# Holding SyncE's transfers back by bytes underway in a four-layer graph kernel

## The chip, the cores and the metric

The kernel runs on one core of a Trainium2 chip. A core has five engines that run side by side and meet at semaphores: TensorE (PE in the profile; its weight loads are PEld), VectorE (DVE), ScalarE (ACT), GpSimd (POOL) and SyncE (SP). Here SyncE does nothing but issue DMA transfers. The metric is device time in microseconds (us); lower is better.

## The reference

There are 128 graphs of 64 nodes with 512 features, so x is 8,192 rows of 512 float32. Four layers follow each other, and each ends in `x = layernorm(x + layer(x, adj))`:

```python
# layer 0: attention over the adjacency, output A @ x @ w
s = (x @ w) @ a;  A = leaky(tanh((s_i + s_j) / 8) * 8);  A = exp(A) * adj, rows scaled
# layer 1: weight = adj * exp(q k^T), rows divided by their sum; output weight @ v
# layer 2: softmax over the nodes of sum(q * (adj @ k)), times v
# layer 3: two hypergraph convolutions with 512 -> 1024 -> 512 features,
#          relu and layernorm between them
```

The weights are the same for all graphs: 512 x 512 for layers 0 to 2 and 512 x 1024, 1024 x 512 for layer 3.

## The kernel before

**Tiles and groups.** Two graphs make a tile of 128 rows, two tiles (`GT`) a group; there are 32 groups (`NG`). `run(g)` adds all operations of group g, in steps 0 to 15: layer 0 in steps 0 to 2, layer 1 in 3 to 6, layer 2 in 7 to 11, layer 3 in 12 to 15. A product with a weight is made of seven block products in place of eight (`seven_products`, Strassen's scheme in Winograd's form). For this each weight is prepared once into seven quarter-size pieces, which are stored in DRAM (`in_dram`), and every group streams them back (`streamed`): w0 for layer 0, v1 and v2 (both "ring<-v" in the profile) for layers 1 and 2, 3a and 3b for layer 3. The pieces go through a ring of eight buffers of 512 KB (kind `ring`). With x, the adjacency and the output this makes some 14 MB a group.

**The planner.** No engine's order is written by hand. The operations are put into a planner (class `Order`), each with an engine, a cost, a key (when it is due) and the buffers that it reads and writes. `Order.run` then plays through the program with its own model of times: an engine that is free takes the ready operation with the smallest key that finds free buffers, and a buffer is taken when its operation starts and is given back when the last one that touches it ends. The order that comes out is what is emitted, engine by engine; on the chip only the semaphores of the data count, not the planner's times. Four groups are worked on at a time (`BASE`, 4 of 16 steps apart), so TensorE has other groups' matmuls to turn to.

TensorE's operations come in the modes "whole" (the array of 128 x 128), "quarters" and "columns" (64 x 64 blocks, divided array), and "any". `choose` prefers to stay in a mode, since a change costs time.

**SyncE in the planner.** A transfer costs SyncE 500 ns (`dma`). A common link moves 300 bytes in a ns, one transfer after another, and 2,200 ns after its end the data counts as landed. The list `landed` keeps these times. When eight transfers are underway (`UNDERWAY`), SyncE is free again only when the eighth from the newest has landed. An operation of SyncE whose key is more than `AHEAD` beyond the earliest unfinished step isn't taken yet.

The key of a ring load is the smallest step of its users less 1.5. x and the adjacency have keys 6 and 7 below their group's base (`load_x`, `load_adj`), so they go out as soon as a buffer of theirs is free. `load_adj` makes one transfer of the adjacency as it is and four small ones that turn it (32 KB each). `load` tells the planner a size of 2 * P * 1024, 256 KB, whatever it loads.

**Waits on the chip.** Each of SyncE's transfers adds to one of eight semaphores, in turn, and waits first for what used the same semaphore before; so on the chip too it can't have more than eight underway. Other waits of SyncE are for buffers: a ring load waits for the matmuls that read its buffer last.

There is one wait that the data doesn't ask for. [...] Where the planner starts a GpSimd operation, it notes in `o.behind` the VectorE operation that had the port before. When the order is emitted, `pinned` gives the next instruction a real wait (a manual dependency of the kind Sync) on the instruction named in the list `behind`, and a NoSync one that fixes its place behind the last of its own engine. `names` remembers the instruction of each operation that could be waited for.

Of the kernel before, what the change touches and what calls it, by code (L numbers as in the profile page):

```python
# [16 lines left out]
P = 128  # L17
B, N, D, DH = 128, 64, 512, 1024
T = B * N // P
GT = 2  # L20
NG = T // GT
CT = 4
# [36 lines left out]
class Order:  # L59
    LATENCY = {"PE": 220, "DVE": 70, "ACT": 60, "POOL": 60, "SP": 2200}  # L60
    BYTES_PER_NS = 300
    UNDERWAY = 8
    TURN, TURN_DIVIDED = 145, 60

    NEAR, FAR = 0.8, 4.0
# [72 lines left out]
    def run(self):  # L138

        ready = {e: [] for e in self.LATENCY}  # L140
        free_at = {e: 0 for e in self.LATENCY}
        number = {o: i for i, o in enumerate(self.ops)}
        events, n, link, mode, burst = [], 0, 0, None, 0
        port_free, port_user, landed = 0, None, []
        for o in self.ops:
            if not o.missing:
                heappush(ready[o.engine], (o.key, number[o], o))
        by_step, front = sorted((o for o in self.ops if o.engine != "SP"), key=lambda o: o.step), 0
        done, now = [], 0
        while len(done) < len(self.ops):  # L150
            moved = False
            while front < len(by_step) and by_step[front].start is not None:
                front += 1
            far = by_step[front].step + self.AHEAD if front < len(by_step) else float("inf")
            for e, heap in ready.items():
                while free_at[e] <= now:
                    skipped, held, found, found_pe = [], set(), None, {}
                    while heap:
                        if e == "SP" and heap[0][0] > far:
                            break  # L160
                        item = heappop(heap)
                        need = defaultdict(int)
                        wants = [b for b in item[2].touches if b.slot is None]
                        for b in wants:
                            need[b.kind] += 1
                        if item[2].port and port_free > now:
                            skipped.append(item)
                        elif all(k not in held and len(self.slots[k]) >= c for k, c in need.items()):
                            if e == "PE":
                                skipped.append(item)  # L170
                                found_pe.setdefault(item[2].mode, []).append((item, wants))
                                if item[0] < 0:
                                    break
                            else:
                                found, takes = item, wants
                                break
                        else:
                            held.update(k for k, c in need.items() if k in held or len(self.slots[k]) < c)
                            skipped.append(item)
                    if found_pe:  # L180
                        found, takes = self.choose(found_pe, mode, burst)
                        skipped.remove(found)
                    for item in skipped:
                        heappush(heap, item)
                    if found is None:
                        break
                    moved, found = True, found[2]
                    turn = 0
                    if e == "PE":
                        if found.mode == "any":  # L190
                            found.mode = "whole" if mode in ("whole", None) else "quarters"
                            found.args = (found.mode == "whole",)
                        if found.mode != mode:
                            turn = self.TURN if "whole" in (found.mode, mode) else self.TURN_DIVIDED
                        mode = found.mode
                        burst = 0 if mode == "whole" else burst + found.matmuls
                    found.start = now
                    done.append(found)
                    found.takes = takes
                    for b in takes:  # L200
                        b.slot = self.slots[b.kind].pop()
                    end = free_at[e] = now + found.cost + turn
                    if found.port:
                        port_free = end
                        if e == "POOL":
                            found.behind = port_user
                        else:
                            port_user = found
                    if e == "SP":
                        link = max(link, now) + found.bytes // self.BYTES_PER_NS  # L210
                        end = max(end, link)
                        landed.append(end + self.LATENCY[e])
                        if len(landed) >= self.UNDERWAY:
                            free_at[e] = max(free_at[e], landed[-self.UNDERWAY])
                    seen = end + self.LATENCY[e]
                    heappush(events, (free_at[e], n, None, None))
                    for u in found.users:
                        n += 1
                        heappush(events, (free_at[e] if u.engine == e and e != "SP" else seen, n, u, None))
                    for b in found.touches:  # L220
                        n += 1
                        heappush(events, (seen, n, None, b))
                    n += 1
            if not events:
                stuck = [(e, h[0][2].key, [b.kind for b in h[0][2].touches]) for e, h in ready.items() if h]
                raise RuntimeError(f"no operation can start: {len(done)} of {len(self.ops)}, {stuck}")
            now = max(now, events[0][0])
            while events and events[0][0] <= now:
                _, _, u, b = heappop(events)
                if u is not None:  # L230
                    u.missing -= 1
                    if not u.missing:
                        heappush(ready[u.engine], (u.key, number[u], u))
                if b is not None:
                    b.left -= 1
                    if not b.left:
                        self.slots[b.kind].append(b.slot)
        return done
# [19 lines left out]
def kernel(  # L258
# [74 lines left out]
    def dma(size, reads, writes, out, in_):  # L333
        order.add("SP", 500, reads, writes, lambda: nc.sync.dma_start(out=out(), in_=in_()), size=size)

    def load(b, src, view=None):
        dma(2 * P * 1024, [], [b], lambda: view(b.t) if view else b.t, lambda: src)

    NOW = 100.0

# [40 lines left out]
    def load_x(g):  # L381
        order.key = BASE[g] - 6.0 if g else -11.0
        xs[g] = Buf("x", 4)
        load(xs[g], x_g[g])

    def load_adj(c):
        order.key = BASE[GC * c] - 7.0 if c else -10.5
        adjs[c] = Buf("adj")
        load(adjs[c], adjT[:, ts(c, CT * N)], lambda t_: t_.rearrange("p t i -> p (t i)"))

        turned = turned_adjs[c] = Buf("adj", 2 * GT)
        for t in range(GT):
            for h in range(2):
                dma(P * 256, [], [turned[2 * t + h]],
                    lambda t=t, h=h: turned.t[ts(t, N)].rearrange("p (g h) i -> p g h i", h=2)[:, :, h],
                    lambda t=t, h=h: adjT_c[c, t][:, :, h])
# [753 lines left out]
    def pinned(engine):  # L1150
        class Pinned:
            def __getattr__(self, name):
                f = getattr(engine, name)

                def call(*args, **kwargs):
                    made = f(*args, **kwargs)  # L1156
                    ins = made.ins
                    key = str(ins.engine)
                    if behind:
                        tc.add_manual_dep(ins, behind.pop(), mybir.DependencyInfo(  # L1160
                            mybir.DependencyClass.Sync, mybir.DependencyReason.DATA), reason="port")
                    if key in last:
                        tc.add_manual_dep(ins, last[key], mybir.DependencyInfo(
                            mybir.DependencyClass.NoSync, mybir.DependencyReason.DATA), reason="order")
                    last[key] = ins.name
                    return made

                return call

        return Pinned()  # L1170
# [7 lines left out]
    for o in order.run():  # L1178
# [2 lines left out]
        if o.behind:  # L1181
            behind.append(names[o.behind])
        o.emit(*o.args)
        if o.port and o.engine == "DVE":
            names[o] = last[str(mybir.EngineType.DVE)]


# [39 lines left out]
```

## Time and profile before

| | |
|---|---|
| median of three runs | 2173.8 us (2173.52 to 2175.92) |
| the profiled execution | 2173.7 us |
| its span, first to last instruction | 2171.8 us |
| mean granted clock of TensorE | 0.997 |
| TensorE busy | 2141.3 us (99%) |
| VectorE, ScalarE, GpSimd busy | 70%, 39%, 18% |
| transfers issued by SyncE | 1,067 |
| moved by DMA | 476 MB, 219 GB/s in the mean |
| share of time that the DMA engines were busy with them | 65.4% |

The busy time of TensorE is made of matmuls whose ends are modelled, so a gap of some 0.1 us between two of them can hide in it. A group of rows names an instruction by what it writes and reads, "bank<-ring,k" being a matmul into a PSUM bank with a ring piece and a buffer of kind k. All instructions carry line 1156, since one helper (`pinned`) emits them. A wait is put down to the engine or transfer whose semaphore came last. "Issue" is time in which the engine waited for nothing that the profile shows.

### The profile page before, as it was taken

The numbers are of one execution on the slowest core, as the hardware profiler recorded it, in microseconds if no ns is written. First come the engines' busy times: TensorE is split into PE (matmuls) and PEld (weight loads), VectorE is DVE, ScalarE is ACT, GpSimd is POOL, SyncE is SP. The second block draws the span as 40 slices with busy tenths as digits, with TensorE's granted clock in tenths as the row PEclk, the third lists the DMA queues.
The fourth block names the chain that finished last, engine by engine and source line by source line (L and its number), as shares of the span: only waits on it lengthen the run. The fifth ranks groups of instructions, "written<-read, shape, count | busy, mean of one in ns | idle before, by whom it ended". The sixth has DMA issues, their size and how long they took to land.

```text
span 2171.8 us, 51970 instructions
## 1 busy us (share of the span) xinstructions
PE 2141.3 (99%) x21079; PEld 1727.3 (80%) x21079; DVE 1531.0 (70%) x3967; ACT 853.1 (39%) x1812; POOL 384.9 (18%) x399
## 2 busy tenths in 40 slices
PE   8999999999999999999999999999999999999998
PEld 4888787887888887877888788878877888888866
DVE  5777767677677777667676676777766767666775
ACT  2444344343343443433433334433434333343333
POOL 1113111021210222201121111212112221012120
PEclk9999999999999999999999999999999999999999
DMA  9776668666666667665666665676656676656475
GB/s 304 232 258 229 210 211 271 213 234 232 216 229 204 205 210 231 233 210 196 205 222 235 210 200 196 220 237 217 223 194 204 222 236 212 210 185 211 158 260 188
DMA packets 174303, 476.38 MB, mean 219 GB/s; under 512 B 35760, under 2 KB 45296, under 8 KB 174064
## 3 DMA queue, kind: packets, MB, share of 16 engines
q1 hardware_dynamic: 174064, 473.05, 65.4%
q8 instruction: 167, 2.74, 0.5%
q14 instruction: 72, 0.59, 0.1%
HBM read 443.33 MB, written 29.66 MB: 218 GB/s over the span
## 4 chain that ended last, share of the span: by engine, by line
PE 99%; issue 1%; DVE 0%; DMA 0%; ACT 0%; SPq 0%; DVEq 0%; ACTq 0%
PE bank L1156 99%; DMA k<-in_wk_dram 0%; DVE col L1156 0%; ACT x L1156 0%; DVE x L1156 0%; ACT k L1156 0%; ACT u_b L1156 0%; SPq L1156 0%; DVE e L1156 0%; DVEq L1156 0%; ACTq L1156 0%
## 5 line engine op out<-in xcount | busy, mean ns | idle before, releaser
L1156 PE MATMUL bank<-ring,k 128*128 128x256 f32 (+1 forms) x3968 | 1037.0, 410 | 5.2 <-issue 4.0
L1156 PEld LDWEIGHTS bank<-ring,k 128*128 128x128 f32 x3968 | 735.1, 191 | 194.9 <-issue 95.3
L1156 DVE SCALAR_TENSOR_TENSOR x<-bank,col,x 128x256 f32<-128x256 f32 (+1 forms) x832 | 399.8, 500 | 223.2 <-PE bank L1156 213.9
L1156 ACT COPY k<-bank 128x512 f32<-128x512 f32 (+1 forms) x640 | 301.6, 503 | 450.0 <-PE bank L1156 363.6
L1156 PEld LDWEIGHTS bank<-k,m 128*128 128x128 f32 x3584 | 429.9, 192 | 23.9 <-issue 10.5
L1156 PE MATMUL bank<-k,m 128*128 128x128 f32 x3584 | 437.1, 275 | 0.0
L1156 PE MATMUL bank<-ring,h 128*128 128x256 f32 (+1 forms) x1408 | 418.4, 439 | 0.0
L1156 POOL TENSOR_TENSOR col<-col,mhalf 128x2 f32<-128x2 f32 (+1 forms) x161 | 111.6, 694 | 1414.1 <-DVE col L1156 913.7
L1156 ACT ACTIVATE x<-x,col,col 128x512 f32<-128x512 f32 x256 | 196.0, 814 | 373.0 <-DVE col L1156 372.9
L1156 PEld LDWEIGHTS bank<-ring,h 128*128 128x128 f32 x1408 | 257.4, 190 | 85.7 <-issue 60.5
L1156 DVE TENSOR_TENSOR k<-bank,k 128x256 f32<-128x256 f32 x384 | 154.0, 421 | 149.4 <-PE bank L1156 147.5
L1156 DVE BATCH_NORM_STATS2 col<-x 128x6 f32<-128x512 f32 x256 | 175.5, 688 | 4.7 <-ACT k L1156 0.3
L1156 ACT ACTIVATE k<-bank,u_c 128x128 f32<-128x128 f32 x256 | 80.3, 366 | 151.0 <-PE bank L1156 140.8
L1156 DVE SCALAR_TENSOR_TENSOR h<-bank,col,b3a_b 128x512 f32<-128x512 f32 x128 | 95.8, 748 | 54.4 <-PE bank L1156 54.2
L1156 DVE TENSOR_TENSOR k<-k 128x256 f32<-128x256 f32 x226 | 103.6, 459 | 34.0 <-ACT k L1156 31.8
L1156 ACT ACTIVATE h<-h 128x512 f32<-128x512 f32 x128 | 80.4, 631 | 107.1 <-DVE h L1156 106.9
L1156 PEld LDWEIGHTS bank<-k,k 128*64 128x64 f32 (+1 forms) x2112 | 77.3, 140 | 51.5 <-DVE k L1156 25.2
L1156 DVE SCALAR_TENSOR_TENSOR h<-bank,col,h 128x512 f32<-128x512 f32 x128 | 93.3, 747 | 31.0 <-PE bank L1156 30.8
L1156 PE MATMUL bank<-k,k 128*64 128x64 f32 (+1 forms) x2112 | 105.5, 238 | 7.0 <-DMA k<-in_wk_dram 6.3
L1156 ACT ACTIVATE h<-h,col,col 128x512 f32<-128x512 f32 x128 | 94.8, 804 | 44.0 <-DVE col L1156 44.0
L1156 POOL TENSOR_TENSOR x<-x,bv_b 128x512 f32<-128x512 f32 x64 | 80.8, 1272 | 107.3 <-PE bank L1156 95.2
L1156 POOL TENSOR_TENSOR k<-k,b3b_b 128x512 f32<-128x512 f32 x64 | 81.4, 1271 | 87.8 <-DVE h L1156 31.1
(98 smaller groups left out, 1493.9 us busy)
## 6 DMA issues: line engine op xcount, KB each, us to landing
ring<-3a SPq DMA_DIRECT2D x224, 512.0 KB, 4.8
ring<-3b SPq DMA_DIRECT2D x224, 512.0 KB, 4.7
ring<-v SPq DMA_DIRECT2D x189, 512.0 KB, 4.2
ring<-w SPq DMA_DIRECT2D x93, 512.0 KB, 3.3
x<-in_x_dram SPq DMA_DIRECT2D x32, 512.0 KB, 4.0
ring<-v SPq DMA_DIRECT2D x63, 256.0 KB, 4.2
out_dram<-x SPq DMA_DIRECT2D x31, 512.0 KB, 5.0
ring<-w SPq DMA_DIRECT2D x31, 256.0 KB, 4.0
```

The costliest lines, as they stand in the source:

```text
L1156: made = f(*args, **kwargs)
```

## The change

Four things are altered.

1. In the planner a second limit stands beside the eight transfers: `BYTES`, 3 << 19, which is 1.5 MB. After each transfer the planner walks back from the newest, starting from 512 KB (1 << 19) for the transfer to come, and adds up sizes. At the first transfer that brings the sum over 1.5 MB, or at the eighth, it stops: SyncE is free again when that one has landed.
2. If it stopped for the bytes, the transfer found is kept in `behind`, and the next transfer of SyncE gets it as `found.behind`. When that one is emitted it has a real wait for the landing, by the way that GpSimd's wait already had. For this `names` keeps SyncE's instructions too.
3. `load` is given the true size: 512 KB for x (P * GT * D * 4), 128 KB for the adjacency (P * CT * N * 4), in place of 256 KB for both.
4. The text that tells the reason of a manual dependency reads "turn" in place of "port".

The planner runs anew with this, so the order of operations on all engines may come out differently.

```diff
-    UNDERWAY = 8
+    UNDERWAY, BYTES = 8, 3 << 19
...
-        port_free, port_user, landed = 0, None, []
+        port_free, port_user, landed, behind = 0, None, [], None
...
                     if e == "SP":
                         link = max(link, now) + found.bytes // self.BYTES_PER_NS
                         end = max(end, link)
-                        landed.append(end + self.LATENCY[e])
-                        if len(landed) >= self.UNDERWAY:
-                            free_at[e] = max(free_at[e], landed[-self.UNDERWAY])
+                        landed.append((end + self.LATENCY[e], found))
+                        found.behind, behind, size = behind, None, 1 << 19
+                        for i, (at, o) in enumerate(reversed(landed), 1):
+                            size += o.bytes
+                            if i == self.UNDERWAY or size > self.BYTES:
+                                free_at[e], behind = max(free_at[e], at), o if i < self.UNDERWAY else None
+                                break
...
-    def load(b, src, view=None):
-        dma(2 * P * 1024, [], [b], lambda: view(b.t) if view else b.t, lambda: src)
+    def load(b, src, size, view=None):
+        dma(size, [], [b], lambda: view(b.t) if view else b.t, lambda: src)
...
-        load(xs[g], x_g[g])
+        load(xs[g], x_g[g], P * GT * D * 4)
...
-        load(adjs[c], adjT[:, ts(c, CT * N)], lambda t_: t_.rearrange("p t i -> p (t i)"))
+        load(adjs[c], adjT[:, ts(c, CT * N)], P * CT * N * 4, lambda t_: t_.rearrange("p t i -> p (t i)"))
...
-                            mybir.DependencyClass.Sync, mybir.DependencyReason.DATA), reason="port")
+                            mybir.DependencyClass.Sync, mybir.DependencyReason.DATA), reason="turn")
...
-        if o.port and o.engine == "DVE":
-            names[o] = last[str(mybir.EngineType.DVE)]
+        if o.engine == "SP" or o.port and o.engine == "DVE":
+            names[o] = last[str(mybir.EngineType.SP if o.engine == "SP" else mybir.EngineType.DVE)]
```

## The prediction

> **What bounds the kernel now.** I read the busy times first, then who TensorE waited for, then SyncE's waits, then SyncE's order around the places where the hold would act.
>
> ```profile
> PE 2141.3 (99%) x21079; PEld 1727.3 (80%) x21079; DVE 1531.0 (70%) x3967; ACT 853.1 (39%) x1812; POOL 384.9 (18%) x399
> ```
>
> TensorE is busy for 99% of the span; 30.5 us are left. The waits of TensorE from 54 us to the end, after the start-up (waiting engine, releaser: us in total, times, longest):
>
> ```profile
> PE bank L1156 <- issue: 13.3, 10, 2.3
> PE bank L1156 <- ACT k L1156: 1.1, 1, 1.1
> PE bank L1156 <- ACT x L1156: 0.2, 1, 0.2
> ```
>
> No transfer is in it (the 1.1 us is one that spills over from 52.84 us). So after the start no matmul is late because of a DMA. The ten waits on "issue" come with the fetch of TensorE's own instructions: each begins between 0.1 us before and 1.6 us after the start of a 16 KB transfer of the instruction queue, and ends 2.2 to 3.0 us after that start. Who SyncE waited for:
>
> ```profile
> SPq L1156 <- PE bank L1156: 1514.0, 772, 11.7
> SPq L1156 <- DMA out_dram<-x: 86.8, 21, 5.7
> ```
>
> For 70% of the span SyncE stands ready and waits until TensorE gives back a ring buffer. Its transfers, KB each and median us to landing:
>
> ```profile
> ring<-3a SPq DMA_DIRECT2D x224, 512.0 KB, 4.8
> ring<-3b SPq DMA_DIRECT2D x224, 512.0 KB, 4.7
> ring<-v SPq DMA_DIRECT2D x189, 512.0 KB, 4.2
> ring<-w SPq DMA_DIRECT2D x93, 512.0 KB, 3.3
> ```
>
> And the one place where TensorE's idle time is in reach of an order of transfers, the end of the start-up:
>
> ```profile
> 51.43 1.41 PE L1156 MATMUL bank<-e,x 64*64 64x64 f32 x64 [1.92 <-DVE e L1156]
> 53.98 2.50 PE L1156 MATMUL bank<-ring,k 128*128 128x256 f32 x5 [1.15 <-ACT k L1156]
> ```
>
> These two waits, 3.1 us, are followed by a clock of one half from 52.2 to 59.0 us: eleven matmuls stand there 0.21 us further from the next than elsewhere, 2.3 us. VectorE and ScalarE end the waits.
>
> **What the Trainium skill says.** "DMA: Bandwidth & Descriptors", Queues, rings and completion order: each DMA engine takes one queue's descriptors in ring order. The trace agrees: the first six 512 KB loads were issued within 3.4 us and landed at 4.79, 6.13, 7.49, 8.84, 10.20 and 11.55 us, one every 1.35 us. The same page, Anatomy of one DMA: a fixed cost of about 2 us lies mostly after the last byte. Here 22 ring loads of 512 KB into an empty queue took 3.19 us (median), which leaves 1.8 us beside the 1.35 us. "Runtime: NRT & Kernel Launch", Instruction fetch mechanics: an engine fetches pages of 256 instructions while it runs the one before. The trace has 167 such transfers and 42,826 weight loads and matmuls, 256 to each.
>
> **The hold itself.** By the new rule SyncE counts 512 KB ahead, then adds transfers from the newest back. With 512 KB each that is 1.0, 1.5, 2.0 MB: the third from the newest must land before the next goes out, so three are underway. Three take 3 x 1.35 = 4.05 us of the queue, and one alone needs 3.19 us, so the queue should not run dry. I applied the rule to the 1,067 issue and landing records. At 308 issues the named transfer had not landed. Moving those issues, and what follows them on SyncE, holds 249 transfers for 237 us in all, but landings move by 0.04 us in the mean and 1.3 us at most, because a transfer that is held would only have stood in the queue. Behind the waiting instruction stand the next loads on SyncE, and TensorE waits for these.
>
> Does anything notice? I laid the kernel's program order of matmuls on the records (all 21,079 match), which gives for each load the time from landing to its first matmul. Of 804 ring loads after 108 us one has 1.1 us (a 3a piece of 177 us), then come 1.6 us and up; 7 more are under 2 us, and all those are first pieces of 3b in a group; ring<-v has a median of 14.5 us. In the moved records these smallest ones are the same. Cost: 0, covered by that slack; if the cover were gone, each late piece would cost its lateness.
>
> **The wait instruction.** Up to 1,056 transfers get a second wait. A lone semaphore wait costs SyncE 0.06 us (20.48 us to the next start at 20.55), so at most 1,056 x 0.06 = 63 us out of its 1514 us of waiting; a piece may land 0.06 us later, against 1.1 us and more. Cost 0. The eighth transfer back is already waited for on the chip (SyncE's transfers use eight semaphores in turn), so the old limit of eight was real too, and 7 stood underway at 50 issues.
>
> **The sizes.** x counts 512 KB instead of 256, the adjacency 128 instead of 256. This moves nothing on the chip. In the planner's link at 300 bytes/ns it is +0.87 us for each of 32 x loads and -0.44 us for each of 16 adjacency loads.
>
> **The order that is planned anew.** Ring loads go out strictly by key: in the records not one of the 804 goes before one with a smaller key. The hold can't reorder them; it can only put x, adjacency and output transfers elsewhere between them. So TensorE's order should stay nearly what it is. Two of its costs can still move. First, 273 changes between whole and divided array: some 250 intervals are longer by 70 to 120 ns, 24.3 us; ten changes more or less are 1.0 us either way. Second, the fetch waits: a page boundary hurts where it meets a burst of 64x64 matmuls. The number of instructions stays but for the operation that goes whole or divided; two waits more or less at 1.33 us are 2.7 us. Together 3.7 us either way, mean 0.
>
> **Start-up.** The first three loads are issued as now, and the first matmul waits for the second of them (6.13 us): 0. The fourth goes out at 4.79 instead of 2.22 us and lands at 4.79 + 0.05 + 3.19 = 8.03 or, queued, 8.84 us as now: 0. The adjacency loads are small, their landing at 14.4 to 15.2 us is set by the queue: 0. The stall at 50 us I leave as it is: the pieces needed at 53.98 us had 2.1 us of slack.
>
> **Sum.** 0 + 0 + 0 + 0 + 0 us: a span of 2171.8 us, with the 1.9 us around it (2173.7 profiled) 2173.7 us; the median of the runs shown is 2173.8. I say 2173.5, taking the nearest half.
>
> **Rivals.** (1) Faster by the start-up: with less in the queue an urgent load passes the prefetches, the waits of 3.1 us and the slow clock of 2.3 us go, and two fetch waits (2.7 us) with them: 8.1 us, 2165.6. For it: the DMA share is 0.98 from 49.5 to 54 us, and a load issued at 50.5 us took 10.1 us. Against: no transfer ended those two waits.
>
> (2) Slower by the 3b pieces. The first two of each group have 1.6 to 3.9 us. If the new plan and the hold together land them later by 2.3 us, the excess over the slack adds up to 4.4 us; by 2.5 us, 8.4 us; by 3.0 us, 24.6 us. It decides from 2.3 us on, and I take 2.5: 2182. For it: the adjacency loads sit between these pieces (828.6 to 832.3 us), and small transfers make the remaining queue short when the hold ends. Against: my replay gives 1.3 us at most, and a held SyncE sends the 3b piece (smaller key) ahead of the adjacency.
>
> (3) That it does nothing on the chip: the wait is a real one, but a third-last landing is mostly past. That has the time of the forecast.
>
> **From cases to numbers.** 0.2% is 4.3 us, about what a measurement of this kernel can tell from no change. Forecast with rival 3, 0.40: 2169.8 to 2177.2. Rival 1, 0.35; it reaches to 2161 if more fetch waits go, at 1.3 us each. Rival 2, 0.25, with a plan that has more changes or fetch waits counted to it on the slow side; it reaches past 2190 with 0.07. The range leaves out 0.07 above 2185 and about 0.10 below 2162. Within 0.2%: 0.38, since the edges of the forecast spill over by 0.02; faster 0.36, slower 0.26.
>
> **What would show it.** Right: SyncE's waits on ring and x landings grow from some 10 to 200 us or more, its waits on TensorE shrink by about as much, the medians to landing of 3a and 3b fall towards 4.1 us, none is above 6 us, and TensorE's waits still name no transfer. Rival 1: the 1.92 and 1.15 us are gone and the clock stays whole at 52 us. Rival 2: TensorE waits on ring<-3b. The forecast is wrong if the plan orders the matmuls differently: then the count of mode changes and the list of "issue" waits will differ by more than ten and two.

## The result: slower by about 1%

| | before | after |
|---|---|---|
| median | 2174.9 us (2173.5 to 2182.0, 4 runs) | 2196.2 us (2193.4 to 2215.1, 4 runs) |
| ratio, 95% interval | | 1.0112 (1.0084 to 1.0141) |
| profiled execution, its span | 2173.7, 2171.8 us | 2193.9, 2191.7 us |
| TensorE busy; mean granted clock | 2141.3 us; 0.997 | 2145.0 us; 0.995 |
| matmul records, mode changes | 21,079, 273 | 21,087, 269 |

A second set of eight executions of the changed kernel (`after_again` below) gave 1.0074 (1.0048 to 1.01). Single executions of one kernel lie some 10 to 20 us apart here, so the verdicts below rest on ratios to the kernel before, executed beside each set, with intervals; a single profile shows the mechanism.

The busy times and the chain of work that ended last, from the page of the changed kernel:

```profile
PE 2145.0 (98%) x21087; PEld 1730.7 (79%) x21087; DVE 1531.7 (70%) x3967; ACT 849.8 (39%) x1812; POOL 386.1 (18%) x399
...
PE 92%; DMA 6%; issue 1%; ACT 1%; SPq 0%; DVE 0%; ACTq 0%; DVEq 0%
```

The amount of work is as before. Before, the chain was 99% TensorE and 0% DMA; now 6% of it are transfers. That isn't a share of time lost: in the stalls described below, the chain runs back from TensorE through ScalarE to late transfers and to the holds ahead of them. SyncE's waits in the changed kernel:

```profile
SPq L1160 <- PE bank L1160: 1003.2, 590, 10.8
SPq L1160 <- DMA ring<-3a: 185.7, 159, 3.8
SPq L1160 <- DMA ring<-3b: 163.6, 125, 3.2
SPq L1160 <- DMA ring<-v: 98.3, 82, 3.3
SPq L1160 <- DMA ring<-w: 97.3, 84, 3.6
```

So the hold is real: 545 us of waiting for landings of ring pieces, taken out of the 1514 us that SyncE used to wait for TensorE. The medians to landing in the page's list of transfers:

```profile
ring<-3a SPq DMA_DIRECT2D x224, 512.0 KB, 4.6
ring<-3b SPq DMA_DIRECT2D x224, 512.0 KB, 4.6
```

They hardly moved: 4.8 and 4.7 us before. TensorE's waits over the whole span are 16.2 us longer in sum, and its busy time, which grows where the clock is halved, is 3.7 us longer; together these are the 19.9 us between the spans. They arise in two places, the first 70 us and the steady state after it. TensorE's waits after 110 us, the longest two (1.6 us more stand below them):

```profile
PE bank L1160 <- issue: 12.6, 8, 3.6
PE bank L1160 <- ACT e L1160: 10.9, 8, 2.5
```

The wait for ScalarE's `e` is new: eight stalls, at 599.65, 864.58, 999.14, 1132.94, 1266.28, 1399.65, 1534.96 and 1669.24 us. They lie some 133 us (or twice that) apart, as the adjacency chunks do: each chunk serves two groups, and eight of the 16 chunks have such a stall. Following TensorE's matmuls group by group, the last matmul of group 4 is 7.8 us later than before (start-up), that of group 10 10.5 us, of group 19 18.4 us, of the last group 20.0 us.

**The start-up.** Stretches of 12 us: their length, then busy us and instructions of PE, PEld, DVE, ACT and POOL, and in the last three columns TensorE's granted clock, DMA share and GB/s. Before:

```profile
12.00:24.00 12.00, 11.70 (x34) 5.45 (x32) 6.56 (x18) 3.11 (x11) 0.00 (x0) 1.00 0.93 311
...
36.00:48.00 12.00, 12.00 (x116) 8.10 (x109) 9.21 (x24) 3.87 (x12) 3.69 (x4) 1.00 0.95 303
```

and after:

```profile
12.00:24.00 12.00, 11.29 (x33) 5.29 (x32) 7.66 (x18) 3.54 (x11) 1.76 (x1) 1.00 0.66 206
...
36.00:48.00 12.00, 11.13 (x44) 6.60 (x36) 8.07 (x19) 1.76 (x6) 1.76 (x1) 1.00 0.66 192
```

From 12 to 24 and from 36 to 48 us the DMA engines lost a third of their throughput. In this stage the weights still have to arrive and be prepared, and what is prepared from a late transfer is late in its turn: over the first 60 us TensorE is busy for 45.5 us, against 50.0 before, and its idle times name VectorE and ScalarE. SyncE's own row of transfers from 12 us on shows how it came about (start, us, transfer, count):

```profile
12.35 3.04 SPq L1160 DMA_DIRECT2D adj<-in_adjT_dram  x5
...
16.55 6.25 SPq L1160 DMA_DIRECT2D k<-in_wqk_dram  x4
```

For 4.2 us, from 12.35 to 16.55, SyncE issues only small transfers, some 0.6 us each. Before the change the same five adjacency transfers took it from 4.97 to 10.80 us, while a backlog of 512 KB loads was still being served. A backlog of at most 1.5 MB is 3 x 1.35 = 4.05 us of the queue; by this sum there is next to none left when SyncE gets through the small ones. That is an argument from the rows; experiment 2 tests it. The rows alone don't show a second cause, a wait for buffers that holds the third and fourth of the wqk loads: it comes out in experiment 1.

**The steady state.** SyncE's transfers around the adjacency chunk that is needed at 865 us, after:

```profile
839.86 0.35 SPq L1160 DMA_DIRECT2D adj<-in_adjT_dram  x1
...
843.77 6.15 SPq L1160 DMA_DIRECT2D ring<-3a  x4
850.80 0.61 SPq L1160 DMA_DIRECT2D adj<-in_adjT_dram  x1
...
854.88 0.60 SPq L1160 DMA_DIRECT2D adj<-in_adjT_dram  x1
857.47 2.05 SPq L1160 DMA_DIRECT2D ring<-v  x2
859.58 2.76 SPq L1160 DMA_DIRECT2D adj<-in_adjT_dram  x2
```

and the answering ones before:

```profile
828.57 1.03 SPq L1156 DMA_DIRECT2D adj<-in_adjT_dram  x2
829.69 0.54 SPq L1156 DMA_DIRECT2D ring<-3b  x1
830.29 1.91 SPq L1156 DMA_DIRECT2D adj<-in_adjT_dram  x3
```

A planner whose SyncE is held finds each time a ring piece with a smaller key ready, so the five transfers of the chunk are strewn over 22 us in place of 4. The last lands at 864.97 us. ScalarE (start, us, operation, and in brackets its idle time before and what ended it), first the copy of the same chunk before, which didn't wait:

```profile
835.96 0.18 ACT L1156 COPY w<-adj 128x4 f32<-128x4 f32 x1
```

and after:

```profile
859.19 0.37 ACT L1160 COPY k<-bank 128x256 f32<-128x256 f32 x1 [0.52 <-PE bank L1160]
865.13 0.20 ACT L1160 COPY w<-adj 128x4 f32<-128x4 f32 x1 [5.57 <-DMA adj<-in_adjT_dram]
865.23 0.58 ACT L1160 COPY k<-bank 128x512 f32<-128x512 f32 x1
865.71 0.52 ACT L1160 ACTIVATE e<-bank,col 128x64 f32<-128x64 f32 x2
```

A copy of 0.2 us (`w <- adj`, the turned adjacency) stood in ScalarE's program for 5.57 us; the copy out of PSUM and the tanh (`e<-bank,col`) behind it could not start. TensorE's next matmul was planned into the PSUM bank that this tanh reads (so in all eight stalls), and waited for it:

```profile
866.28 2.94 PE L1160 MATMUL bank<-k,m 128*128 128x128 f32 x24 [1.71 <-ACT e L1160]
```

The Trainium skill says so: in "Perfetto Trace Analysis", Tensor Engine Instruction (MATMUL, LD_WEIGHTS), the ScalarE, VectorE and GpSimd queues are strictly first in, first out. This trace agrees for ScalarE: nothing passed the copy in these 5.57 us.

### The profile page after: what moved, and what is told of

It is laid out like the page before. It is cut to its first block, busy times and chain, and to the rows that moved or that the text cites. A ratio compares the mean times of both kernels' runs of the same rounds, so it can differ in the third digit from the quotient of the medians.

```text
span 2191.7 us, 52074 instructions
## 1 busy us (share of the span) xinstructions
PE 2145.0 (98%) x21087; PEld 1730.7 (79%) x21087; DVE 1531.7 (70%) x3967; ACT 849.8 (39%) x1812; POOL 386.1 (18%) x399
## 4 chain that ended last, share of the span: by engine, by line
PE 92%; DMA 6%; issue 1%; ACT 1%; SPq 0%; DVE 0%; ACTq 0%; DVEq 0%
PE bank L1160 92%; DMA ring<-3a 2%; DMA ring<-v 2%; DMA adj<-in_adjT_dram 1%; SPq L1160 0%; ACT k L1160 0%; DMA k<-in_wqk_dram 0%; DMA k<-in_wk_dram 0%; DMA w<-ring 0%; DMA ring<-in_wv_dram 0%; DMA ring<-3b 0%; ACT e L1160 0%; DMA v<-ring 0%; ACT x L1160 0%; DVE col L1160 0%
## 5 line engine op out<-in xcount | busy, mean ns | idle before, releaser
L1160 PE MATMUL bank<-k,m 128*128 128x128 f32 x3584 | 439.6, 276 | 10.9 <-ACT e L1160 10.9
L1160 DVE TENSOR_TENSOR k<-k 128x256 f32<-128x256 f32 x226 | 95.0, 421 | 23.8 <-ACT k L1160 22.2
```

## The experiments

All the kernels compute what the two above do; they differ in orders and waits alone, and one is the changed kernel again. The first theory was A: the new order costs, not the waits.

**1. The plan without the wait.** SyncE's instructions get no extra wait; all orders are those of the changed kernel.

```diff
-        if o.behind:
+        if o.behind and o.engine != "SP":
             behind.append(names[o.behind])
```

> The changed kernel with its planned order, but SyncE's new wait is not emitted. Theory A (the order costs the time: the small adjacency transfers are planned behind ring loads, and ScalarE's copy of them stands without slack and blocks ScalarE): most of the loss stays, 2183 to 2195 us, and ScalarE still waits for adjacency transfers for 25 us or more. Rival B (the real wait on the chip costs it): back to 2172 to 2179 us, ScalarE's waits for the adjacency under 10 us.

Measured: 2182.4 us, ratio 1.0027 (1.0014 to 1.0041). The order by itself costs, though less than the whole change. In its profile the start-up is slow again (group 5 ends 10.6 us later than before), and the DMA queue has a hole from 12 to 24 us without any hold on the chip:

```profile
12.00:24.00 12.00, 12.00 (x35) 5.64 (x33) 6.66 (x17) 2.94 (x10) 1.77 (x1) 1.00 0.51 163
```

SyncE's waits up to 60 us show the cause:

```profile
SPq L1160 <- PE bank L1160: 8.1, 2, 6.5
```

The planner's orders and buffers explain these two waits. The old plan put all four wqk loads into buffers that nothing had used yet. In the new plan the third and fourth go out later, and get the buffers of the two wq pieces, which the planner by then believes to be free. On the chip TensorE still reads them: the third load goes out at 21.42 us, 0.03 us after the last of these matmuls has ended, and the four loads take SyncE from 14.07 to 23.62 us. The changed kernel has the same plan and the same two waits (4.4 us; third and fourth load at 20.60 and 22.43 us, against 14.87 and 15.38 before). So the plan alone makes a hole from 12 to 24 us. It doesn't make the one from 36 to 48 us, where the DMA share of this run is 0.99.

TensorE waits for `e` only 0.2 us here: without the waits the adjacency lands some 2.5 us after ScalarE is ready for the copy, in the median chunk, against 4.7 us in the changed kernel.

**2. The wait without the plan.** All orders are those of before, on all engines; each transfer of SyncE gets the wait that the 1.5 MB rule with true sizes (`o.true`) gives for that order.

```diff
+                        went.append(found)
+                        found.behind, behind, size = behind, None, 1 << 19
+                        for i, o in enumerate(reversed(went), 1):
+                            size += o.true
+                            if i == self.UNDERWAY or size > 3 << 19:
+                                behind = o if i < self.UNDERWAY else None
+                                break
```

> The kernel before with its own order, sizes and limits in the planner, and on top the real waits by the 1.5 MB rule (with true sizes) for SyncE. Theory A: 2172 to 2180 us, nothing in the steady state. Rival B: 2190 to 2200 us. If the start-up alone is hurt by the wait, 2178 to 2183 us with the loss before 110 us.

Measured: 2188.3 us, 1.0049 (1.0029 to 1.0068). Theory A in its first form fell, and so did the prediction's "Start-up ... 0": waits alone, in the old order, cost about 11 us. The place is the start-up: the DMA share is 0.78 from 12 to 24 us and 0.68 from 36 to 48 us (0.93 and 0.95 before), though no load waits for a buffer of wq here. In the order of before, the fifth transfer lands 0.75 us late, the wqk loads 2.9 us, the first ring<-w piece 10.1 us (60.04 against 49.95). TensorE's waits on transfers in this run name the ring now (6.4 us):

```profile
PE bank L1164 <- DMA ring<-w: 6.4, 3, 4.7
```

and its matmuls show where:

```profile
60.17 2.04 PE L1164 MATMUL bank<-ring,k 128*128 128x256 f32 x4 [4.67 <-DMA ring<-w]
```

Group 0 ends 10.2 us later than before, group 11 12.3 us, the last one 14.0 us. So some 10 of the 14 us are lost in the start-up.

**3. The true sizes without the limit.**

```diff
-    UNDERWAY, BYTES = 8, 3 << 19
+    UNDERWAY, BYTES = 8, 1 << 40
```

> The changed kernel with the limit of bytes out of reach, so that only the true sizes of x and of the adjacency are left (and the eight transfers). Theory A: 2171 to 2180 us, since the turned adjacency transfers go out together again, some 1 us of planned slack for ScalarE's copy. If the sizes were the cause: 2190 us or more.

Measured: 2175.4 us, 1.0001 (0.9984 to 1.0019). The sizes cost nothing. What I hadn't expected is in ScalarE's waits of this run:

```profile
ACT w L1160 <- DMA adj<-in_adjT_dram: 135.3, 11, 15.2
```

ScalarE stands for the adjacency two and a half times as long as in the changed kernel (54.6 us), and TensorE doesn't notice: its waits after 54 us are 12.6 us of fetch, 1.4 and 0.2. ScalarE's wait took the place of another (for VectorE's `col`, 372.9 us before, 252.6 here). A blocked engine costs only where urgent work stands behind it.

**4. The change, with ScalarE's copy placed later.** The planner takes a landing 3 us later where a ScalarE operation waits for it.

```diff
-  heappush(events, (free_at[e] if u.engine == e and e != "SP" else seen, n, u, None))
+  heappush(events, (free_at[e] if u.engine == e and e != "SP" else seen + (e == "SP" and u.engine == "ACT") * 3000, n, u, None))
```

The orders of TensorE, VectorE, GpSimd and SyncE come out exactly as in the changed kernel, and so do all of SyncE's waits; 110 of ScalarE's 1,811 operations stand in another place.

> The changed kernel, but the planner counts a landing 3 us later where a ScalarE operation waits for it, so that ScalarE's copy of the adjacency is placed some 3 to 4.5 us later in ScalarE's order; hold and waits stay. Theory A: the eight waits of TensorE on ScalarE go (11 to 12 us), the start-up loss of about 8 us stays: 2179 to 2186 us. Rival B, or any cause that is not ScalarE's blocked queue: 2191 us or more.

Measured: 2179.5 us, 1.0010 (0.9993 to 1.0026). Moving these few operations of one engine that is 39% busy gives back nearly all of the loss. The start-up stays slow (groups 5 to 11 end 9.6 to 9.9 us later than before), but the last group ends only 3.5 us later. TensorE's waits for its own instructions after 110 us, 9.4 us against 12.3, are a part of what shrank the delay; the rest isn't traced. ScalarE at the same chunk:

```profile
862.40 0.58 ACT L1160 COPY k<-bank 128x512 f32<-128x512 f32 x1 [3.50 <-PE bank L1160]
862.88 0.52 ACT L1160 ACTIVATE e<-bank,col 128x64 f32<-128x64 f32 x2
...
865.84 0.18 ACT L1160 COPY w<-adj 128x4 f32<-128x4 f32 x1
```

The copy out of PSUM and the tanh now stand ahead of `w <- adj`, which finds its data there. TensorE's wait on `e` is gone from the list.

In the planner's own times the copy started 2.8 us after the planned landing in most chunks before, and with no margin at all in 15 of 16 chunks after; here it is 3 us or more. The plan reckoned 2.7 us from issue to landing for such a small transfer; on the chip the middle half of them takes 3.4 to 4.4 us in the changed kernel after 450 us.

**5 to 8. Start-up and steady state apart.** The limit, in the planner and as waits, acts only before or only after 110 us of planned time, and the latter also with ScalarE's copy 3 us later as in 4. The changed kernel was repeated beside them.

```diff
-                            if i == self.UNDERWAY or size > self.BYTES:
+                            if i == self.UNDERWAY or size > self.BYTES and now < 110000:
```

> The changed kernel with the hold (plan and wait) only for the planner's first 110 us; true sizes; after that only the eight transfers. Theory C (two separate losses: the queue runs dry in the start-up, 8 to 10 us; and ScalarE's blocked queue in the steady state, 11 to 12 us): the start-up loss alone, 2180 to 2187 us (ratio 1.003 to 1.006), no waits of TensorE on ScalarE e after 450 us. Rival (one cause, that goes on through the whole run): about half of it or more stays in the steady state however the start went; here then less than 3 us lost.

Measured: 2189.9 us, 1.0052 (1.0031 to 1.0074).

> The changed kernel with the hold (plan and wait) only after the planner's first 110 us. Theory C: the loss up to 110 us goes (within 2 us of before there), and the waits of TensorE on ScalarE stay with 8 to 14 us: 2184 to 2192 us (ratio 1.004 to 1.008). If the start-up were the whole cause: 2173 to 2179 us.

Measured: 2192.6 us, 1.0064 (1.004 to 1.0088). TensorE waits 8.6 us for `e`, in 8 waits; the start-up is as fast as before (group 4 ends 2.7 us earlier).

> As late_110, and the planner counts a landing 3 us later where a ScalarE operation waits for it. Theory C: both losses are away, 2171 to 2180 us (ratio 0.998 to 1.002), though SyncE waits for some 300 us or more for landings. If the waits of SyncE cost anything more in the steady state, 2183 us or more.

Measured: 2179.3 us, 0.9997 (0.9982 to 1.0013). Only ScalarE's order differs from the run ahead of it. SyncE's waits in this run:

```profile
SPq L1160 <- DMA ring<-3a: 191.0, 170, 3.6
SPq L1160 <- DMA ring<-3b: 179.6, 131, 3.8
```

The hold is as strong as in the changed kernel, and costs nothing measurable. In the steady state the waits themselves are free, as the prediction had it.

> The changed kernel as it is, on the same chip as the three beside it. Both theories: 1.008 to 1.014 of the kernel before.

Measured: 2194.2 us, 1.0074 (1.0048 to 1.01).

**9. The early limit with ScalarE's copy later.** `early_110` with the edit of 4.

> early_110 (bytes limit, in the planner and as waits, in the first 110 us only) with the landings that ScalarE waits for taken 3 us later in the planner. Four of the five engines have the order of early_110 without any difference; 56 of ScalarE's 1,811 operations stand elsewhere. Theory A (the start-up's loss is a queue that runs dry under the hold, and has nothing to do with ScalarE): it loses like early_110, a ratio of 1.003 to 1.006, groups 5 to 12 end 8 to 12 us later than in before, DMA share under 0.75 from 12 to 24 and from 36 to 48 us. Rival B (early_110 lost by ScalarE's 154 us of waiting for the adjacency): ScalarE's wait for it falls under 20 us and the ratio is 1.000, within 0.0015.

Measured: 2183.6 us, 1.0023 (1.0009 to 1.0037), between what the two theories expected. The start-up alone costs, with ScalarE out of the way, about 5 us: group 5 ends 12.6 us later than before, the last one 9.5 us, and the DMA share from 12 to 24 and from 36 to 48 us is 0.67 and 0.69. ScalarE's wait for the adjacency is 0.6 us. Whether some of what `early_110` lost was ScalarE's is not shown: the two intervals overlap, and its profiled execution (2181.4 us), the fastest of its six, shows no wait of TensorE on `e` over 0.3 us.

**10. Two MB in place of 1.5.**

```diff
-    UNDERWAY, BYTES = 8, 3 << 19
+    UNDERWAY, BYTES = 8, 4 << 19
```

> The limit is 2 MB in place of 1.5 MB, in the planner and as real waits; nothing else is changed. Four loads of 512 KB can then be underway. The planner's orders come out as in sizes_only but for 43 of SyncE's 1,067 places, all before the 275th, and 17 of ScalarE's; the planned margin of ScalarE's copy behind the adjacency is 0.7 us, as against 0 under 1.5 MB and 1.1 in sizes_only. Theory A (what costs is a queue that runs dry in the start-up and a ScalarE that stands behind the adjacency; the real waits in themselves cost nothing): both are smaller, the DMA share from 12 to 48 us is 0.85 or more, group 5 ends less than 5 us later than in before, TensorE waits less than 3 us for ScalarE's e, ratio 0.999 to 1.003. Rival B (each real wait costs, or any limit by bytes does): ratio 1.005 or more.

Measured: 2176.9 us, 0.9995 (0.9981 to 1.0008). The stretches of the start-up:

```profile
12.00:24.00 12.00, 11.31 (x34) 5.39 (x33) 6.95 (x19) 3.54 (x11) 0.00 (x0) 1.00 0.84 286
...
36.00:48.00 12.00, 12.00 (x45) 8.00 (x44) 9.33 (x25) 2.87 (x11) 2.58 (x3) 1.00 0.92 278
```

With one more load underway the queue runs dry far less (DMA share 0.84, 0.96 and 0.92 in the three stretches, the first a hair below what was expected), group 5 ends 1.3 us earlier than before, and TensorE waits for `e` 0.3 us. SyncE still waits 50.2 us for 3b and 34.5 us for 3a landings. So it isn't a limit by bytes that costs, but this one's size. This run doesn't tell the two causes of the start-up apart: its plan also gives the wqk loads unused buffers again (the third goes out at 15.43 us).

The ratios to before, side by side:

| the 1.5 MB limit acts | ScalarE's copy as planned | 3 us later |
|---|---|---|
| all the time | 1.0112 and 1.0074 | 1.0010 |
| in the first 110 us | 1.0052 | 1.0023 |
| after 110 us | 1.0064 | 0.9997 |

From the last row: in the steady state ScalarE's order costs 0.6%, and only together with the waits, since `plan_only` has the same order and stalls of 0.2 us. From the right column: the start-up costs 0.1 to 0.2% with ScalarE's order mended, and the interval of the first (0.9993 to 1.0026) reaches below 1, so for it no loss is shown. None of the versions beats the kernel before: 0.9995 and 0.9997 are equal to it.

## Why the prediction was wrong

It said 2173.5 us, 2162 to 2185; it is 2196.2.

- **"The hold itself", steady state: right.** TensorE waits for no ring piece, and all of 806 ring loads after the start land 0.56 us or more ahead of their first matmul. The holds were more and longer (450 waits and 545 us, not 249 and 237 us), the replay having been of the old order, but `late_110_act3` shows that they cost nothing. The medians to landing fell to 4.6, not to 4.1 us.
- **"Three take 3 x 1.35 = 4.05 us of the queue, and one alone needs 3.19 us, so the queue should not run dry", and "Start-up ... 0": wrong.** This compared landings of 512 KB loads alone. It left out SyncE's own time for small transfers, 0.4 to 0.6 us each and 3 us or more for `mask_rows`, in which a queue with 1.5 MB drains. The moved records gave landings 0.04 us later in the mean, where `wait_only`, in the same order, has the first ring<-w piece 10.1 us late. In the changed kernel a 512 KB load with two others of 512 KB underway took 4.9 us to land in the median (322 loads; middle half 4.5 to 5.4), not 4.05, so a chain of holds moves less than one load every 1.35 us. Nor did the prediction see that a load planned later can get another buffer, and wait for it (experiment 1). Priced by the runs, both causes together: 0.1 to 0.5%, 2 to 11 us.
- **"The order that is planned anew": the step that failed in the steady state.** That ring pieces go ahead of the adjacency was seen ("a held SyncE sends the 3b piece (smaller key) ahead of the adjacency"), and counted as a point against a loss. I laid slack on the transfers that TensorE waits for; the adjacency is waited for by ScalarE, and its margin was never looked at. The term that was missing: 8 stalls of TensorE, 10.9 us in sum. Measured alone, by `late_110` and `late_110_act3`, it is 0.64% less -0.03%: some 14 us, of which the stalls of that run are 8.6 us; half-clock windows and fetch waits that differ between the two profiles are in the rest, which isn't traced.
- **"TensorE's order should stay nearly what it is": not quite.** 249 of TensorE's 2,276 operations stand in another place. The signs named for that, ten changes or two fetch waits more or less, didn't show it. An order that differs as much need not cost: `sizes_only`, where 191 operations stand elsewhere, is at 1.0001.
- **The ± 3.7 us for mode changes and fetch waits: held.** 273 changes became 269, fetch waits 13.3 us became 12.6. Between versions the fetch waits went from 9.4 to 17.7 us. Two labels of the prediction are off and move no term: of the 273 changes 212 are between whole and divided array (206 after), the others between the two divided modes; and 42,826 counts 668 waits and drains beside the weight loads and matmuls.
- **"The sizes" and "The wait instruction": right.** `sizes_only` is 1.0001, `late_110_act3` 0.9997.
- **The rivals.** That of late 3b pieces had the sign, not the mechanism: TensorE never waits for 3b. The start-up was named as a chance to be faster; it was slower. That the wait does nothing is out.

The profile had what was needed. ScalarE's list of waits of before has, far down, one entry for a transfer:

```profile
ACT w L1156 <- DMA adj<-in_adjT_dram: 1.6, 1, 1.6
```

Sixteen copies need the adjacency, and one of them waited 1.6 us. For eleven of the others the last transfer had landed less than 1 us before ScalarE was ready for them: a margin that is nearly used up. After:

```profile
ACT w L1160 <- DMA adj<-in_adjT_dram: 54.6, 12, 10.1
```

## What to carry to other kernels

A limit on transfers underway must cover the longest stretch in which the issuing engine sends only small ones, not just the latency of a large one. A planner that sends a load later may also give it another buffer: look up who still reads that one. When a change makes some transfers give way, look up who waits for those, and what stands behind the waiter in its own program: an engine at 39% can hold up one at 99%. A planner that puts an in-order engine's instruction exactly at a planned landing turns each microsecond of a late transfer into a stall.

## What the runs showed of the hardware

- A stall can cost more than itself. After the stall of 1.92 us at 1399.65 us TensorE's clock is at one half for 3.41 us, from 1403.05 to 1406.46 us. No rule comes out of these traces: of the eight stalls for `e` this is the only one so followed; the longest, 2.52 us at 599.65 us, and a fetch wait of 3.64 us at 339.71 us were not. Fetch waits of 1.84 us (at 1898.60 us) and, before, of 2.31 us (at 2148.14 us) were. The Trainium skill, in "TensorE: Matmul & The Clock Gate", What's actually happening, gives windows of 3413 ns and says that the clock drops after at least one idle window; the length agrees, but here single gaps of around 2 us were enough.
- Issuing takes SyncE's own time, and not by size: 0.32 us for a ring piece of 512 KB, 0.61 us for a turned adjacency transfer of 32 KB (medians), 3.0 to 3.9 us for the one store of `mask_rows`, whose data was ready before.
- With the same order of instructions on TensorE (changed kernel and `act_late3`) the fetch waits were 12.6 and 9.4 us: where they fall depends on timing as well as on the order.
